# Sums of the exponentials in a second attention layer: one running tile, and the product with ones and the division each a step later

## The chip, the cores and the metric

The kernel runs on one core of one Trainium2 chip. The metric is the device time in microseconds (us), smaller is better. A time is a median of runs; beside it stands one profiled execution, from which all durations come.

## What is computed

Two cross-attention layers, in fp32, over 4 batches of 1024 rows of width 512. Cut to what matters here, layer 1 is:

```python
xn = x * rsqrt(mean(x * x) + 1e-5) * norm_w
q = rotate(xn @ wq)            # 16 heads of 32
k, v = rotate(ctx @ wk), ctx @ wv
q, k = q / norm(q), k / norm(k)
attn = softmax(q @ k.T * sqrt(32))
out = x + (attn @ v) @ wout
```

Since q and k are normalised, no maximum is subtracted: the kernel takes exp(scores), multiplies by v, and divides at the end by the sum of the exponentials over all 1024 keys. That sum, for each query and head, is what the change is about. Layer 0 (16 heads of 64) is not edited.

## The kernel before, in words

The program is one long order of instructions for the engines, written out by hand: TensorE (PE) for all products and transposes, ScalarE (ACT) for exponentials and for most copies out of PSUM, VectorE (DVE) for maxima, adds, rotations and divisions, GpSimd (POOL) for small powers and some products, SyncE (SP) for transfers. Each engine works through its instructions in the order in which the code issues them; between engines there are semaphore waits.

The batches follow each other, and in each layer 0 comes before layer 1. PE's free time in an attention step is filled with other products, called units here: a queue `Units` holds functions with estimated costs, `fill(us)` runs so many of them, and a few due times (`until`) force them.

Layer 1 has, for each batch, two halves (of 8 heads each) of 8 blocks; a block is 256 queries (`qb`) of 4 heads (`g`), and has 4 steps (`kk`), each for 256 keys. A half so has 32 steps, a batch 64, and the kernel 64 blocks. `Attention1.step` (from L594) does, in this order:

- 16 score matmuls (L599, four heads side by side in the array) into two PSUM tiles; there are two such buffers, both used by one step, so that the scores of the next step wait for the exponentials of this one.
- two exponentials on ACT (L609) into `self.e[:, kk % 2]`; the tile has two places, so an exponential waits until the product and the adds of two steps ago have read its place.
- `self.finish()` (L611): the division left over from before, and `product` of the step before: 8 value matmuls (L638) into the PSUM tile `av` (tag f0). At a block's end it adds 8 matmuls with a tile of ones (L649), for the running sum and for the last pair-sum, into the second half of the same PSUM bank. One ACT copy (L653) takes both halves out; the division (reciprocal L656, product L657) is left for the next step.
- `self.u.fill(us)`: units. In a first half these are the projections of q, k and v of layer 1 with their transposes; in a second half the output of layer 1 (`po`) and the next batch's preparation.
- on DVE, two adds (L615), which add the two key tiles of a step's exponentials, into `both[:, kk]`, and for kk = 1 and 2 a running add (L619) into `both[:, 0]`.

The function `bank` gives a unit one of three PSUM banks in turn during layer 1 (f1 to f3). A unit that gets a bank waits until what was in it has been read. A q or k projection is read by ACT (a square, L499) and by DVE (L501 to L503), which with L504 and L506 are called the rotation here; then POOL (L508, L512) finishes it and a transpose follows two chains later (L521). The function `post` runs at once in layer 1, so the rotation stands on DVE ahead of the adds of the step in which the projection ends.

In the last batch's second half the blocks are sorted so that o[2] is complete first, and the products with the last half of `wout` (`adds`) are put into the queue at fixed steps; what is left runs after the loop (`tail`).

Of the kernel before, what the change touches and what calls it, by code (L numbers as in the profile page):

```python
# [30 lines left out]
F32 = mybir.dt.float32  # L31
# [4 lines left out]
P = 128  # L36
S = 1024
NT = S // P
# [8 lines left out]
HD1 = 32  # L47
# [60 lines left out]
def xattn_kernel(ctx: ExitStack, tc: tile.TileContext, a: dict, out: bass.AP):  # L108
    nc = tc.nc
# [6 lines left out]
    ps_f = ctx.enter_context(tc.tile_pool(name="ps_f", bufs=1, space=bass.MemoryType.PSUM))  # L116
# [7 lines left out]
    def bank(name):  # L124

        which["n"] = which["n"] + 1 if which["n"] < 3 else which["from"]
        return ps_f.tile([P, 512], F32, tag=f"f{which['n']}", name=name)
# [7 lines left out]
    ones = const.tile([P, HD1], F32, name="ones")  # L135
# [224 lines left out]
    class Attention0:  # L360


        def __init__(self, b, units):
            self.b, self.u = b, units
            self.blocks = deque()
# [209 lines left out]
    WQ = 256  # L575

    class Attention1:


        def __init__(self, b, units):  # L580
            self.b, self.u = b, units
            self.last = None
            self.av = None
            self.quotient = None
            self.e = sb.tile([P, 2, 2, 2, 2, WQ], F32, tag="e", bufs=2, name=f"e1_{b}")
            self.both = sb.tile([P, 4, 4, WQ], F32, tag="big", bufs=2, name=f"both_{b}")
            rest = sb.tile([P, 4, 1024], F32, tag="big", bufs=2, name=f"rest_{b}")
            self.avs = rest[:, 0].rearrange("p (n c q) -> p n c q", n=2, c=2)
            v1 = rest[:, 2:].rearrange("p g (t f) -> p g t f", f=P)
            self.v1 = [v1[:, g] for g in range(2)]  # L590

        def step(self, half, g, qb, kk, kT, qT, v, o, us):
            n = f"{self.b}_{half}_{g}_{qb}_{kk}"
            sc = [score(f"s1_{n}_{u}", (P, 2, 2, WQ)) for u in range(2)]  # L594
            for c in range(2):
                for j in range(4):
                    rr = slice(j * HD1, (j + 1) * HD1)
                    k = 2 * kk + c
                    nc.tensor.matmul(  # L599
                        sc[j // 2][:, j % 2, c, :],  # L600
                        kT[rr, g, k * P : (k + 1) * P],
                        qT[rr, g, qb * WQ : (qb + 1) * WQ],
                        start=True,
                        stop=True,
                    )
            es = []
            for u in range(2):
                e = self.e[:, kk % 2, u]
                nc.scalar.activation(e, sc[u], AF.Exp, scale=float(np.sqrt(np.float32(HD1))))  # L609
                es.append(e)  # L610
            self.finish()  # L611
            self.last = (half, g, qb, kk, v, es, o)
            self.u.fill(us)
            for u in range(2):
                nc.vector.tensor_add(  # L615
                    self.both[:, kk, 2 * u : 2 * u + 2, :], es[u][:, :, 0, :], es[u][:, :, 1, :]
                )
            if 0 < kk < NT // 2 - 1:
                nc.vector.tensor_add(self.both[:, 0], self.both[:, 0], self.both[:, kk])  # L619

        def finish(self):

            if self.quotient is not None:
                self.quotient()
                self.quotient = None
            if self.last is not None:
                self.product()

        def product(self):
            half, g, qb, kk, v, es, o = self.last  # L630
            n = f"{self.b}_{half}_{g}_{qb}"
            if kk == 0:
                self.av = ps_f.tile([P, 2, WQ], F32, tag="f0", name=f"av1_{n}")
            first, end = kk == 0, kk == NT // 2 - 1
            for c in range(2):
                for j in range(4):
                    rr = slice(j * HD1, (j + 1) * HD1)
                    nc.tensor.matmul(  # L638
                        self.av[rr, 0, :],
                        v[g][:, 2 * kk + c, rr],  # L640
                        es[j // 2][:, j % 2, c, :],
                        start=first and c == 0,
                        stop=end and c == 1,
                    )
            if end:
                for i in (0, NT // 2 - 1):
                    for j in range(4):
                        rr = slice(j * HD1, (j + 1) * HD1)
                        nc.tensor.matmul(  # L649
                            self.av[rr, 1, :], ones, self.both[:, i, j], start=i == 0, stop=i > 0  # L650
                        )
                s = self.avs[:, qb % 2]
                nc.scalar.copy(s, self.av)  # L653

                def divide():
                    nc.vector.reciprocal(s[:, 1, :], s[:, 1, :])  # L656
                    nc.vector.tensor_mul(o[g][:, qb * WQ : (qb + 1) * WQ], s[:, 0, :], s[:, 1, :])  # L657

                self.quotient = divide
            self.last = None  # L660


# [5 lines left out]
    def flat(lists):  # L668
        return [u for lst in lists for u in lst]
# [54 lines left out]
    work = Units()  # L724
# [15 lines left out]
    tail = []  # L740
    for b in range(B):
# [6 lines left out]
        for p in range(NPAIR):  # L748
# [15 lines left out]
            elif p % 2 == 0:  # L764
                i = p // 2 - 1
# [4 lines left out]
                    lambda n, i=i: wo[i][:, n % 2, :],  # L770
# [29 lines left out]
            for i in range(NT):  # L800
# [8 lines left out]
                n = NT * (NPAIR - p if later else 1) - i  # L809
# [30 lines left out]
        att1 = Attention1(b, work)  # L840
# [10 lines left out]
        for half in range(2):  # L851
            n = 0
            if half == 0:
                vs = value_chains(att1.v1, wv1, ct, f"pv1_{b}_1")
                first = [q[1], (norms[1]["stats"], [], []), vs[0], (norms[1]["apply"], [], k1[1][2]), k1[2]]
                rest = [(norms[1]["turn"] + q[2][0], [], q[2][2]), k1[3], q[3], q1[0], vs[1], q1[1], q1[2]]
                rest += [q1[3], vs[2], vs[3]]
                chains = first + rest
                work.add(weave(chains, 2))
                def mark(c):  # L860

                    i = chains.index(c)
                    return sum(len(x[0]) for x in chains[: i + 3]) + sum(len(x[2]) for x in chains[: i + 1])

                base = work.done
                marks = {8: base + mark(q[1]), 16: base + mark(rest[0]), 24: base + mark(q[3])}
            else:
                for g in range(2, 4):
                    o[g] = sb.tile([P, S], F32, tag="vals", bufs=4, name=f"o1_{b}_{g}")
                wo1 = [wo_load(a["wout"], i, f"wo1_{b}_{i}") for i in range(2)]  # L870
                adds = add_units(xt, lambda n: o[n], lambda n: wo1[0][:, n % 2, :], f"po1_{b}_0", (0, 1))
                if b + 1 < B:
                    st, order = prepare_units(b + 1)
                    work.add(order(adds))
                else:
                    work.add(flat(adds))
            blocks = [(qb, g) for qb in range(S // WQ) for g in range(2)]
            final = b == B - 1 and half == 1
            if final:
                blocks.sort(key=lambda block: block[1])  # L880
                adds = [
                    add_units(
                        xt, lambda n: o[n], lambda n: wo1[1][:, n % 2, :], f"po1_{b}_{i}", (i,), store if i == 3 else None
                    )
                    for i in (2, 3)
                ]
            for qb, g in blocks:
                for kk in range(NT // 2):
                    if half == 0 and n in marks:
                        work.until(marks[n])  # L890
                    if final and n == 18:
                        work.add(flat(adds[0]))
                    if final and n in (22, 26, 30):
                        work.add(flat(adds[1][(n - 22) // 2 : (n - 18) // 2]))
                    att1.step(half, g, qb, kk, kT, qT, v, o[2 * half :], work.total() / (32 - n))
                    n += 1
            work.drain()
            kT, qT, v = kT1, qT1, att1.v1
        att1.finish()
        att1.quotient()  # L900
        which["from"], which["cols"] = 0, 1
        if b == B - 1:
            tail = flat(adds[1][6:])
        else:
            outs = add_units(
                xt, lambda n, o=o: o[n], lambda n, w=wo1[1]: w[:, n % 2, :], f"po1_{b}_1", (2, 3), store
            )
            tail = flat(outs)
# [38 lines left out]
```

## Time and profile before

| what | value |
|---|---|
| median of 3 runs (lowest, highest) | 2992.65 us (2991.08, 2992.93) |
| profiled execution: time, span | 2989.95 us, 2987.7 us |
| granted PE clock in it, mean | 0.996 |
| steps of layer 1, first half of batch 0 | 511.4 to 643.3 us |
| steps of layer 1, second half of batch 0 | 643.3 to about 775 us |
| steps of layer 1, last half of the last batch | 2864.5 to about 2974 us |

How to read it: the span is the time of the profiled execution between its first and last instruction. A row of a group gives the line in the code, engine, operation, output<-input, shapes and count, then the busy time in us, the mean of one in ns, and the engine's idle time just before these with what ended it. PEld is the load of weights, beside PE. A matmul in fp32 is two records. In the timeline a row has start, length, engine, line and operation, and in brackets the idle time of its engine before it. In the sums by stretch the values are the length, the busy time of each engine with its number of instructions, the granted clock, and the transfers. In a row of waits stand the sum, the number and the longest.

### The profile page before, as it was taken

The numbers are of one execution on the slowest core, as the hardware profiler recorded it, in microseconds if no ns is written. First come the engines' busy times: TensorE is split into PE (matmuls) and PEld (weight loads), VectorE is DVE, ScalarE is ACT, GpSimd is POOL, SyncE is SP. The second block draws the span as 40 slices with busy tenths as digits, with TensorE's granted clock in tenths as the row PEclk, the third lists the DMA queues.
The fourth block names the chain that finished last, engine by engine and source line by source line (L and its number), as shares of the span: only waits on it lengthen the run. The fifth ranks groups of instructions, "written<-read, shape, count | busy, mean of one in ns | idle before, by whom it ended". The sixth has DMA issues, their size and how long they took to land.

```text
span 2987.7 us, 60793 instructions
## 1 busy us (share of the span) xinstructions
PE 2917.3 (98%) x24748; PEld 1544.2 (52%) x24748; DVE 2230.7 (75%) x2824; ACT 1429.5 (48%) x2265; POOL 416.6 (14%) x392
## 2 busy tenths in 40 slices
PE   8999999999999999999999999999999999999998
PEld 5544546555544555655554454555455445455544
DVE  4777795877777779587777777958777777795777
ACT  3444443666443444465644344446664444444664
POOL 0010022420000002232000000223200000022310
PEclk9999999999999999999999999999999999999999
DMA  5788674010387867301048776730104978772000
GB/s 148 169 192 180 158 178 112 22 35 25 81 203 185 186 163 171 94 21 35 25 98 207 175 183 166 171 84 21 35 25 113 205 176 182 170 169 69 2 2 30
DMA packets 374134, 348.50 MB, mean 117 GB/s; under 512 B 37600, under 2 KB 355296, under 8 KB 373856
## 3 DMA queue, kind: packets, MB, share of 16 engines
q1 hardware_dynamic: 371664, 343.43, 48.4%
q8 instruction: 197, 3.23, 0.5%
q10 hardware_dynamic: 2192, 1.19, 0.2%
q14 instruction: 81, 0.66, 0.1%
HBM read 67.64 MB, written 8.39 MB: 25 GB/s over the span
## 4 chain that ended last, share of the span: by engine, by line
PE 78%; DVE 10%; DMA 4%; SPq 3%; ACT 2%; issue 1%; POOL 1%; DVEq 0%; ACTq 0%
PE s L372 14%; PE av L451 13%; PE po L158 10%; PE pv L158 7%; PE s L599 7%; PE av L638 6%; PE pqT L158 6%; PE pkT L158 5%; PE q_p L158 3%; DMA eT<-e 2%; SPq L406 2%; PE av L649 2%; DVE both L615 2%; DVE e L399 2%; PE k_p L158 1%; DVE m L393 1%
## 5 line engine op out<-in xcount | busy, mean ns | idle before, releaser
L394 ACT ACTIVATE e<-s,m 128x1024 f32<-128x1024 f32 x512 | 565.6, 1109 | 679.2 <-DVE m L393 613.8
L393 DVE TENSOR_REDUCE m<-s 128x1 f32<-128x1024 f32 x512 | 602.8, 1219 | 320.0 <-PE s L372 320.0
L399 DVE STREAM_TRANSPOSE e<-e 128x1024 f32<-128x1024 f32 x512 | 606.7, 1224 | 54.9 <-ACT e L394 43.0
L609 ACT ACTIVATE e<-s 128x1024 f32<-128x1024 f32 x512 | 496.5, 1022 | 315.1 <-PE s L599 300.1
L372 PE MATMUL s<-qk 64*128 64x512 f32 x2048 | 520.5, 615 | 6.0 <-ACT e L394 5.3
L451 PE MATMUL av<-eT,v 128*64 128x256 f32 x4096 | 474.8, 385 | 15.6 <-DMA eT<-e 13.7
L615 DVE TENSOR_TENSOR both<-e 128x512 f32<-128x512 f32 x512 | 342.4, 701 | 127.7 <-ACT e L609 92.5
L451 PEld LDWEIGHTS av<-eT,v 128*64 128x64 f32 x4096 | 289.4, 138 | 214.0 <-issue 53.7
L372 PEld LDWEIGHTS s<-qk 64*128 64x128 f32 x2048 | 181.8, 186 | 262.6 <-issue 188.9
L599 PE MATMUL s<-q,k 32*128 32x256 f32 x4096 | 305.7, 402 | 5.8 <-ACT q L526 2.7
L599 PEld LDWEIGHTS s<-q,k 32*128 32x128 f32 x4096 | 191.6, 185 | 149.7 <-ACT e L609 71.4
L158 PE MATMUL po<-wo,vals 128*128 128x512 f32 x512 | 239.6, 601 | 2.5 <-ACT v L130 2.5
L158 PE MATMUL pqT<-hT,w 128*128 128x512 f32 (+1 forms) x800 | 241.3, 597 | 0.7 <-ACT hT L255 0.7
L443 ACT COPY vals<-rT 128x256 f32<-128x256 f32 x128 | 47.7, 372 | 327.4 <-PE rT L442 327.4
L301 DVE TENSOR_TENSOR x<-x,po 128x512 f32<-128x512 f32 x200 | 133.8, 679 | 82.8 <-PE po L158 82.8
L158 PEld LDWEIGHTS pv<-w,cT 128*128 128x128 f32 (+1 forms) x2400 | 176.7, 152 | 30.3 <-issue 27.2
L158 PE MATMUL pv<-w,cT 128*128 128x128 f32 (+1 forms) x2400 | 186.5, 275 | 0.0
L158 PE MATMUL pkT<-cT,w 128*128 128x512 f32 (+1 forms) x600 | 181.6, 599 | 1.1 <-ACT cT L130 1.1
L619 DVE TENSOR_TENSOR both<-both 128x1024 f32<-128x1024 f32 x128 | 159.7, 1248 | 4.4
L158 PEld LDWEIGHTS po<-wo,vals 128*128 128x128 f32 x512 | 90.9, 190 | 106.4 <-issue 101.4
L158 PEld LDWEIGHTS pqT<-hT,w 128*128 128x128 f32 (+1 forms) x800 | 85.9, 151 | 112.2 <-issue 105.9
L638 PE MATMUL av<-e,v 128*32 128x256 f32 x2048 | 137.0, 385 | 0.0
(461 smaller groups left out, 2667.0 us busy)
## 6 DMA issues: line engine op xcount, KB each, us to landing
eT<-e SPq DMA_DIRECT2D x2048, 128.0 KB, 2.8
xr<-in_x_dram SPq DMA_DIRECT2D x32, 256.0 KB, 4.3
x<-in_x_dram SPq DMA_DIRECT2D x32, 256.0 KB, 3.8
wo<-in_Wo_dram SPq DMA_DIRECT2D x16, 512.0 KB, 4.2
out_dram<-x SPq DMA_DIRECT2D x32, 256.0 KB, 2.7
w<-in_Wq_dram SPq DMA_DIRECT2D x31, 256.0 KB, 4.0
c<-in_ctx_dram SPq DMA_DIRECT2D x32, 192.0 KB, 4.5
wkv<-in_wkv_dram SPq DMA_DIRECT2D x16, 384.0 KB, 3.5
```

What stands on the lines that cost most here:

```text
L158: nc.tensor.matmul(o[rr], lhsT[:, rr], rhs, start=start, stop=stop)
L301: nc.vector.tensor_add(xt[t], xt[t], pp[0])
L372: nc.tensor.matmul(sc[j][:, kb * 512 : (kb + 1) * 512], pr["qT"][r[j], i * P : (i + 1) * P], pr["kT"][r[j], kb * 512 : (kb + 1) * 512], st ...
L393: nc.vector.tensor_reduce(m[:, j : j + 1], sc[j], AX.X, ALU.max, negate=True)
L394: nc.scalar.activation(e[j], sc[j], AF.Exp, bias=m[:, j : j + 1], accum_out=l[:, j : j + 1])
L399: nc.vector.transpose(e[j], e[j])
L451: nc.tensor.matmul(av[r[j], :W].rearrange("p (t a i) -> p t a i", t=BQ, a=4), pr["v"][:, k, r[j]], eT[:, j, :, :, k * 32 : (k + 1) * 32], ...
L599: nc.tensor.matmul(sc[j // 2][:, j % 2, c, :], kT[rr, g, k * P : (k + 1) * P], qT[rr, g, qb * WQ : (qb + 1) * WQ], start=True, stop=True,)
L609: nc.scalar.activation(e, sc[u], AF.Exp, scale=float(np.sqrt(np.float32(HD1))))
L615: nc.vector.tensor_add(self.both[:, kk, 2 * u : 2 * u + 2, :], es[u][:, :, 0, :], es[u][:, :, 1, :])
L619: nc.vector.tensor_add(self.both[:, 0], self.both[:, 0], self.both[:, kk])
L638: nc.tensor.matmul(self.av[rr, 0, :], v[g][:, 2 * kk + c, rr], es[j // 2][:, j % 2, c, :], start=first and c == 0, stop=end and c == 1,)
```

## The change

- At each step the two pair-adds go into a tile `part` (into `total` at the block's first step), and at each later step, the last one too, `part` is added to `total`. `total` and `part` alternate between two places by blocks. A block so has three running adds instead of two.
- The product with ones takes `total` alone: 4 matmuls instead of 8. It isn't in the block's last `product` any more, but a function `sums`, called by `finish` a step later, ahead of that step's value product. It writes into a bank that `bank` gives, one of the three of the units, and a second ACT copy takes it out.
- The division follows a step after that.
- `av` has a bank to itself, and its copy takes only the values.
- In the last half the products of the last output begin two steps later, and four, not two, units of the last group come after the loop. Three calls of `finish` end a batch.

```diff
@@ step
             self.finish()
             self.last = (half, g, qb, kk, v, es, o)
             self.u.fill(us)
+            total, part = (self.both[:, 2 * (self.n % 2) + i] for i in range(2))
             for u in range(2):
-                nc.vector.tensor_add(
-                    self.both[:, kk, 2 * u : 2 * u + 2, :], es[u][:, :, 0, :], es[u][:, :, 1, :]
-                )
-            if 0 < kk < NT // 2 - 1:
-                nc.vector.tensor_add(self.both[:, 0], self.both[:, 0], self.both[:, kk])
+                to = (part if kk else total)[:, 2 * u : 2 * u + 2, :]
+                nc.vector.tensor_add(to, es[u][:, :, 0, :], es[u][:, :, 1, :])
+            if kk:
+                nc.vector.tensor_add(total, total, part)
@@ finish
             if self.quotient is not None:
                 self.quotient()
                 self.quotient = None
+            if self.sums is not None:
+                self.sums()
+                self.sums = None
             if self.last is not None:
                 self.product()
@@ product
             if end:
-                for i in (0, NT // 2 - 1):
-                    for j in range(4):
-                        rr = slice(j * HD1, (j + 1) * HD1)
-                        nc.tensor.matmul(
-                            self.av[rr, 1, :], ones, self.both[:, i, j], start=i == 0, stop=i > 0
-                        )
                 s = self.avs[:, qb % 2]
-                nc.scalar.copy(s, self.av)
+                nc.scalar.copy(s[:, 0, :], self.av[:, :WQ])
+                total = self.both[:, 2 * (self.n % 2)]
+                self.n += 1
 
                 def divide():
                     nc.vector.reciprocal(s[:, 1, :], s[:, 1, :])
                     nc.vector.tensor_mul(o[g][:, qb * WQ : (qb + 1) * WQ], s[:, 0, :], s[:, 1, :])
 
-                self.quotient = divide
+                def sums():
+                    ps = bank(f"sums_{n}")
+                    for j in range(4):
+                        rr = slice(j * HD1, (j + 1) * HD1)
+                        nc.tensor.matmul(ps[rr, :WQ], ones, total[:, j], start=True, stop=True)
+                    nc.scalar.copy(s[:, 1, :], ps[:, :WQ])
+                    self.quotient = divide
+
+                self.sums = sums
@@ xattn_kernel, layer 1
-                    if final and n == 18:
+                    if final and n == 20:
                         work.add(flat(adds[0]))
-                    if final and n in (22, 26, 30):
-                        work.add(flat(adds[1][(n - 22) // 2 : (n - 18) // 2]))
+                    if final and n in (24, 28):
+                        work.add(flat(adds[1][(n - 24) // 2 : (n - 20) // 2]))
@@
-        att1.finish()
-        att1.quotient()
+        for _ in range(3):
+            att1.finish()
@@
-            tail = flat(adds[1][6:])
+            tail = flat(adds[1][4:])
```

More of the change, by code (lines that the diff above doesn't have):

```diff
@@ L583, in __init__ @@
             self.av = None
-            self.quotient = None
+            self.sums = self.quotient = None
+            self.n = 0
             self.e = sb.tile([P, 2, 2, 2, 2, WQ], F32, tag="e", bufs=2, name=f"e1_{b}")
@@ L632, in product @@
             if kk == 0:
-                self.av = ps_f.tile([P, 2, WQ], F32, tag="f0", name=f"av1_{n}")
+                self.av = ps_f.tile([P, 2 * WQ], F32, tag="f0", name=f"av1_{n}")
             first, end = kk == 0, kk == NT // 2 - 1
@@ L638, in product @@
                     nc.tensor.matmul(
-                        self.av[rr, 0, :],
+                        self.av[rr, :WQ],
                         v[g][:, 2 * kk + c, rr],
```

## The prediction

> **What bounds the kernel now.** I read the page's first part, then the sums by stretch, then the groups of instructions and the waits of PE, and last the timeline around the longest of those waits.
>
> ```profile
> PE 2917.3 (98%) x24748; PEld 1544.2 (52%) x24748; DVE 2230.7 (75%) x2824; ACT 1429.5 (48%) x2265; POOL 416.6 (14%) x392
> ```
>
> PE sets the time over the whole span. The change touches layer 1 only, so I look there: first half of batch 0, its second half, and the second half of the last batch (us, then the busy time of PE, PEld, DVE, ACT, POOL).
>
> ```profile
> 511.00:645.00 134.00, 127.52 (x1940) 71.87 (x1944) 102.86 (x144) 83.89 (x112) 48.28 (x31) 0.99 0.06 17
> 645.00:777.00 132.00, 131.73 (x1960) 69.24 (x1952) 93.65 (x129) 81.88 (x99) 3.74 (x4) 1.00 0.13 39
> 2866.00:2987.00 121.00, 111.73 (x1408) 52.99 (x1400) 93.44 (x122) 66.92 (x73) 0.00 (x0) 0.99 0.05 19
> ```
>
> A second half with a next batch has no idle PE; a first half has 6.5 us, the last one 9.3. DVE, at 77%, 71% and 77%, is the second engine. What the change edits (all lines), and PE's waits:
>
> ```profile
> L615 DVE TENSOR_TENSOR both<-e 128x512 f32<-128x512 f32 x512 | 342.4, 701 | 127.7 <-ACT e L609 92.5 <-PE av L649 35.2
> L619 DVE TENSOR_TENSOR both<-both 128x1024 f32<-128x1024 f32 x128 | 159.7, 1248 | 4.4
> L656 DVE RECIPROCAL rest<-rest 128x256 f32<-128x256 f32 x64 | 111.9, 1748 | 11.3 <-ACT rest L653 9.9
> L649 PE MATMUL av<-both,ones 128*32 128x256 f32 x1024 | 80.3, 383 | 15.4 <-DVE both L615 15.4
> ```
>
> ```profile
> PE av L649 <- DVE both L615: 15.4, 9, 2.2
> ...
> PE pth L253 <- DVE rot L503: 6.7, 4, 1.7
> ```
>
> The first is the wait that the change aims at, the second a wait for a filler bank that DVE still reads. Step 28 of the first half of batch 0 (counted from 0, it starts at 623.76) shows how the first comes about:
>
> ```profile
> 625.23 0.68 DVE L501 TENSOR_TENSOR rot<-q_p,cos 128x512 f32<-128x512 f32 x1
> ...
> 627.82 2.51 DVE L615 TENSOR_TENSOR both<-e 128x512 f32<-128x512 f32 x4
> ...
> 628.56 1.24 PE L649 MATMUL av<-both,ones 128*32 128x256 f32 x6 [2.22 <-DVE both L615]
> ```
>
> And the sums by stretch for the time just after it (the value after POOL's is PE's granted clock):
>
> ```profile
> 630.00:632.00 2.00, 2.00 (x24) 1.50 (x17) 1.44 (x2) 0.58 (x1) 1.92 (x2) 0.50 0.00 0
> ```
>
> A rotation stands on DVE ahead of the adds; the sums product waits; and PE then runs at half clock, 0.50. Step 28 takes 8.65 us (623.76 to 632.40). Its work is 4.22: from starts in an undisturbed step (543.88, 544.95, 545.84, 546.70), scores 1.07, product 0.88, sums product 0.86, and three filler groups of 0.47. So 4.4 us are lost.
>
> [...] a gap of 2.22 us suffices here: of nine PE gaps over 2.1 us in the timeline, six are followed by half clock; none of 1.67 or less is. A drop costs 1.7 us. [...] each rotation on DVE (L501) starts just after ACT's square (L499) ends, 559.69 and 559.76 for one. [...] L619's typical one takes 1225. [...] the L619 at 620.90, beside POOL's L512, took 1.95 us.
>
> **The change part by part.** A batch has 64 steps, 32 per half, and a block is four; the sums of a block fall 7 times in a first half and 9 times in a second, its end included (L649 has 112 and 144 records there, 16 each).
>
> *Sums product, 8 matmuls to 4.* 0.86 to 0.43 us: a first half saves 3.0, a second 3.9. All of it is on PE.
>
> *Third running add per block.* 64 x 1.225 = 78 us on DVE, 9.8 per half: DVE would be busy 113 us in a first half whose PE work is about 118. It lies beside PE work only as long as DVE is not late.
>
> *Sums a step later.* The wait on the last pair-add goes, and DVE no longer waits for L649 (35.2 us). In its place the sums wait for the whole running total, queued behind whatever DVE has. Behind them on PE wait the value product and all fillers.
>
> *Division another step later.* Same 2.17 us, now at the third step of a block, ahead of that step's rotation and adds.
>
> *Copies.* One of 0.586 becomes two of 0.38 (L568's 128x256 form): ACT +0.17 x 64 = 11 us. ACT is at 62%; if that cover fails, a square behind the copy starts 0.4 later, which I count at step 17 below.
>
> *The sums take a filler bank.* Three banks go round. The order in which the built program issues instructions shows PE waits on DVE and ACT that were not there, where a sum comes between two projections: the second transpose of step 6, the value projection of step 17, the second q projection of step 22 now ask for the bank of a projection that has just ended.
>
> *Last half.* Output units start two steps later and four, not two, run after the last step, with their adds and stores on DVE and SP; the first two now fill PE's 3.02 us wait for the last division.
>
> First half, walked by hand from the trace's durations (adds 1.25 per step, running add 1.15, rotation 2.6, division 2.1, as they follow each other on DVE), in us:
> - Step 4 waits for POOL's rotation at 529.43 in any case: the 0.86 saved there is lost again, +0.86.
> - Step 6: bank free 5.26 into the step, PE there at 2.97: 2.3 (before 1.65).
> - Step 12: 2.5 before, gone. But DVE then holds division, three pair-adds, three running adds and two rotations in a row; the total of step 11 ends at about 567.1, the sums of step 13 are reached at 564.1: 3.0.
> - Steps 16, 20, 28: 0.84, 0.42 and 4.43 before, gone.
> - Step 17: product and sums end the projection at 584.96, the transpose ends at 585.55, the rotation has read the bank at about 587.4: 1.85, new. Step 22: 604.13 against 606.03: 1.9, new. Step 29: sums late by 0.7.
>
> Before 9.83, after 9.75 + 0.86 = 10.6. With the 3.0 of work a first half gains 2.2; four, 9. The 9.83 hold their lost clock; the new ones do not. I give a drop 0.75 for step 13, 0.4 for step 6, 0.15 each for 17 and 22: 1.45 x 1.7 = 2.5, times four: 10 back. Bounds: no drop, or all 16, 27 us. First halves: **+1**.
>
> Second halves with a next batch: 3.9 less 0.9 for bank waits and for the total at the batch's end (it ends at 774.41, where the product before it ends near 774.1): 3.0 x 3 = **-9** (bounds -12 and -4).
>
> Last half: steps 0 to 19 are paced from exponential to exponential, and each block's L649 lies in a pace (4.19 instead of 3.32); the four sums moved lie under a 2.77 pace that has room. 5 x 0.87 = 4.4, and less to wait in the first block 0.2. In the last twelve steps (2929.5 to 2974.3, 44.8) PE work falls by 3 x 0.43 + two units of 0.87 = 3.0; DVE there needs about 42.7, near the bound. The tail loses about 0.1 by the running add against the filled gap. **-7.5** (bounds -10 and -2).
>
> Sum: 1 - 9 - 7.5 = -15.5. Against the profiled execution (2989.95, span 2987.7): 2974.5. The median of the runs is 2.7 above that execution, so **2977**.
>
> **Rivals.** *The total is in time.* If DVE, freed of its waits for L649, is early by 3 us at step 13, the waits of 13 and 29 go. Speaks for it: 31 us idle DVE in a first half. Against: at that place DVE is gapless from 552 to 565 already. Per first half 10.6 - 3.7 = 6.9 against 9.83, and 3.0 of work: -5.9, four -24, no drops; with -16.5: 2952.
> *The bank wait becomes the bound.* DVE's queue doesn't drain, each of the 12 bank waits grows by one running add, 12 x 1.225 = 15, and every wait costs clock, 27: -9 + 42 - 16.5 = +16.5, so 3009. It decides from the point where a first half waits, clock included, over 7 us more than before. For it: three waits lie at 1.85 to 2.3, close to the 2.1 from which clock is lost. Against: 1.67 cost none.
> *Nothing changes.* Waits only move, and the 0.43s go into exponentials' pace: 2992.
>
> **Chances.** Forecast 0.50 (of this 0.36 faster, 0.10 same, 0.04 slower; its own range 2966 to 2996), total in time 0.24, bank wait 0.22, nothing 0.04. About 0.2% (6 us) is what a measurement of this kernel can tell from no change. Faster 0.60, same 0.14, slower 0.26. Range 2948 to 3010: it takes in the middle of the two rivals and leaves some 0.08 below and 0.10 above.
>
> **What would show it.** L649's successor with 512 records and waits of PE for the running add (3 us at step 13, not at step 12); new PE waits on L503 of about 2 us at steps 17 and 22; DVE above 110 us in a first half; half clock after step 13. It would be wrong if no PE wait on L503 appears beside step 6, if DVE is never a step behind, or if second halves don't shorten by 3 us each.

## The result, and the profile after

The changed kernel takes 3011.24 us, the median of seven runs (3001.69 to 3015.06). Seven runs of the kernel before, made beside them on the same chip, give 2991.10 (2988.97 to 2997.24). The medians are 20 us apart; the ratio over all runs is 1.0051, interval 1.0035 to 1.0068, which is 15 us. It is slower, where I had forecast 15 us less. The seven runs of the changed kernel lie in two groups, three near 3002 and four from 3011 to 3015, and the profiled one (3013.35) is of the upper group.

The first part of the page after shows the work that was taken from PE and given to DVE: 524 PE records fewer (512 of the sums; 12 because two more output units run after the loop, as one matmul each instead of four), 64 more DVE instructions, 83 us more DVE work. (A matmul is two records; a step has 8 score matmuls in 16 records, not 16 matmuls as said above.)

```profile
PE 2911.9 (97%) x24224; PEld 1537.8 (51%) x24224; DVE 2313.5 (77%) x2888; ACT 1428.6 (47%) x2329; POOL 421.8 (14%) x392
```

The sums by stretch come next: the first half of batch 0, its second half, and the end of the last batch (length, busy time of PE, PEld, DVE, ACT and POOL, granted clock, transfers).

```profile
514.00:652.00 138.00, 124.93 (x1856) 69.73 (x1856) 112.55 (x150) 82.22 (x117) 49.12 (x31) 0.95 0.05 16
652.00:782.00 130.00, 128.60 (x1908) 67.50 (x1906) 103.82 (x138) 82.77 (x110) 3.74 (x4) 1.00 0.12 35
2889.00:3011.00 122.00, 111.82 (x1380) 53.62 (x1372) 107.10 (x134) 69.90 (x87) 0.00 (x0) 0.97 0.05 19
```

The second half got shorter and has hardly any idle PE. The first half got longer: PE is idle for 13 us of it, and its granted clock is 0.95, where it was 0.99. The following table sets the stages of the two profiled executions side by side. A stage's length is taken from one step's start to the next in the trace; "half" is the time in it that the clock stands at half.

| stage | before, us | half | after, us | half | difference |
|---|---|---|---|---|---|
| layer 0, four batches | 1941.4 | 10.2 | 1949.0 | 27.2 | +7.6 |
| first halves, four | 526.4 | 10.2 | 552.8 | 58.1 | +26.4 |
| second halves, three | 396.7 | 0 | 389.4 | 0 | -7.3 |
| last half with the tail | 123.2 | 3.9 | 119.9 | 8.6 | -3.3 |

So most of the loss lies in the first halves. Three things make up the 26.4 us there. PE is idle for 51.7 us (length less busy time), where it was for 24.2: 27.5 more. PE is busy for 52.7 of the 58.1 us at half clock, where it was busy for all of the 10.2; the clock is 0.50 there, and the value product takes 1.93 us instead of 1.07 (both below). If half of the busy time is lost, this is up to 21 us more, an estimate from these numbers. What is left of the sum, about 22 us, is work that PE was spared; 12 of it are the four products of 28 blocks (0.43 us each), and where the rest comes from was not traced. So the new waits alone take up the gain, and the clock makes it a loss.

The groups of instructions that the change made, by shape:

```profile
L618 DVE TENSOR_TENSOR both<-e 128x512 f32<-128x512 f32 x512 | 345.4, 706 | 92.2 <-ACT e L610 87.3
L620 DVE TENSOR_TENSOR both<-both 128x1024 f32<-128x1024 f32 x192 | 237.4, 1236 | 6.6
...
L663 PE MATMUL sums<-both,ones 128*32 128x256 f32 x512 | 43.4, 413 | 26.1 <-DVE both L620 26.1
```

The sums product is halved (512 records, 43.4 us, where L649 had 1024 and 80.3), and DVE no longer waits for PE ahead of a pair-add: the 35.2 us put down to L649 are gone from the row of L618. In their place the row of L663 has 26.1 us of idle PE. The waits of PE (sum, number, longest) put it in order:

```profile
PE sums L663 <- DVE both L620: 26.1, 16, 4.4
PE q_t L521 <- POOL rot L512: 9.4, 4, 2.3
...
PE pth L253 <- DVE rot L503: 7.9, 4, 2.0
PE q_p L158 <- DVE rot L503: 7.9, 4, 2.0
PE pv L158 <- DVE rot L503: 7.3, 4, 1.8
```

Before, the first and the last two rows didn't exist; L649's 15.4 stood in their place, the third was 6.7 and the second 2.3. Each of the last four comes once per first half, always at the same step. The timeline around the longest wait of a first half, step 13 of batch 0, shows how it comes about:

```profile
562.84 1.75 DVE L656 RECIPROCAL rest<-rest 128x256 f32<-128x256 f32 x1
...
567.09 1.23 DVE L620 TENSOR_TENSOR both<-both 128x1024 f32<-128x1024 f32 x1
...
568.24 0.68 DVE L501 TENSOR_TENSOR rot<-k_p,cos 128x512 f32<-128x512 f32 x1
...
570.82 1.28 DVE L618 TENSOR_TENSOR both<-e 128x512 f32<-128x512 f32 x2
...
572.13 1.22 DVE L620 TENSOR_TENSOR both<-both 128x1024 f32<-128x1024 f32 x1
...
573.41 1.08 PE L663 MATMUL sums<-both,ones 128*32 128x256 f32 x8 [3.74 <-DVE both L620]
...
574.27 1.93 PE L642 MATMUL av<-e,v 128*32 128x256 f32 x16
```

Among what follows on DVE are a division, a running add, a rotation, a pair-add and the third running add of the block. The sums stand for 3.74 us at the head of PE's queue, and the value product that comes behind them then takes 1.93 instead of 1.07. The sums by stretch of the same place show the clock (the value after POOL's):

```profile
572.00:579.00 7.00, 5.58 (x56) 2.56 (x56) 6.93 (x8) 1.93 (x3) 3.99 (x2) 0.52 0.00 0
```

The clock is 0.52: half clock began at 572.3, inside the wait, and lasted 6.83 us. Step 13 takes 11.19 us in all.

### The profile page after: what moved, and what is told of

It reads as the page before. It is cut to its first block, busy times and chain, and to the rows that moved or that the text cites. A ratio compares the mean times of both kernels' runs of the same rounds, so it can differ in the third digit from the quotient of the medians.

```text
span 3011.1 us, 59861 instructions
## 1 busy us (share of the span) xinstructions
PE 2911.9 (97%) x24224; PEld 1537.8 (51%) x24224; DVE 2313.5 (77%) x2888; ACT 1428.6 (47%) x2329; POOL 421.8 (14%) x392
## 4 chain that ended last, share of the span: by engine, by line
PE 76%; DVE 12%; DMA 4%; ACT 3%; SPq 2%; issue 2%; POOL 1%; ACTq 0%; DVEq 0%
PE s L372 14%; PE av L451 13%; PE po L158 10%; PE s L600 7%; PE pv L158 7%; PE pqT L158 6%; PE av L642 6%; PE pkT L158 4%; PE q_p L158 3%; DMA eT<-e 2%; DVE both L618 2%; DVE both L620 2%; PE k_p L158 2%; SPq L406 2%; DVE e L399 1%
## 5 line engine op out<-in xcount | busy, mean ns | idle before, releaser
L618 DVE TENSOR_TENSOR both<-e 128x512 f32<-128x512 f32 x512 | 345.4, 706 | 92.2 <-ACT e L610 87.3
L600 PE MATMUL s<-q,k 32*128 32x256 f32 x4096 | 313.6, 408 | 4.5 <-ACT q L526 2.7
L620 DVE TENSOR_TENSOR both<-both 128x1024 f32<-128x1024 f32 x192 | 237.4, 1236 | 6.6
L158 PEld LDWEIGHTS pv<-w,cT 128*128 128x128 f32 (+1 forms) x2400 | 176.7, 152 | 30.3 <-issue 27.2
L642 PE MATMUL av<-e,v 128*32 128x256 f32 x2048 | 145.4, 404 | 0.0
```

The costliest lines, as they stand in the source:

```text
L158: nc.tensor.matmul(o[rr], lhsT[:, rr], rhs, start=start, stop=stop)
L600: nc.tensor.matmul(sc[j // 2][:, j % 2, c, :], kT[rr, g, k * P : (k + 1) * P], qT[rr, g, qb * WQ : (qb + 1) * WQ], start=True, stop=True,)
L618: nc.vector.tensor_add(to, es[u][:, :, 0, :], es[u][:, :, 1, :])
L620: nc.vector.tensor_add(total, total, part)
L642: nc.tensor.matmul(self.av[rr, :WQ], v[g][:, 2 * kk + c, rr], es[j // 2][:, j % 2, c, :], start=first and c == 0, stop=end and c == 1,)
```

## The experiments

Theory A says that the turn of the filler banks is the cause: the sums take one of three banks that go round, so all units behind them come back to a bank one unit earlier, while DVE still reads it. Theory B says that the late total is the cause: the third running add, on an engine that has fallen behind, stands at the head of PE's queue. None of the kernels below leaves out a part of the computation. The first four were made with 35 runs of the kernel before (median 2991.84), the last four with 11 (2988.67); the ratios are to these.

**The sums out of the turn.** The kernel after, but the sums use the bank that is next without moving the turn on.

```diff
                 def sums():
+                    kept = which["n"]
                     ps = bank(f"sums_{n}")
+                    which["n"] = kept
```

> The changed kernel, but the sums' bank doesn't move the turn of the three filler banks (the next unit takes the same bank). Theory A (the loss comes from PE gaps and the half clock after them; the gaps at steps 6, 17 and 22 of a first half from the shifted turn of banks): step 6 back to a gap of 1.7 us, no gaps on L503 at 17 and 22, no half clock after 6 and 17; per first half 0.3 + 1.8 + 2.0 + 3.4 = 7.5 us less, 30 in all, about 2980. Theory B (the loss is DVE's 78 us of added adds, the banks only show it): the waits move to the sums or the exponentials, time within 6 us of the changed kernel, 3003 to 3012.

Measured: 2994.51 us, ratio 1.0007 (0.9994 to 1.0020), so about 17 us of the 20 came back by the medians, 13 of 15 by the ratio. PE's waits in its profile:

```profile
PE sums L665 <- DVE both L620: 26.3, 20, 4.4
...
PE pth L253 <- DVE rot L503: 6.2, 4, 1.5
...
PE q_p L158 <- ACT rest L666: 3.4, 4, 0.9
```

The bank waits of steps 17 and 22 are gone, that of step 6 is back to 1.5, and a small new one appears, of a unit that takes the bank which ACT still copies the sums from (0.86 us each). The wait for the total is untouched, at 3.74 in step 13, and so is the half clock after it. So A's part is worth most of the net loss. B may still be worth more than the few us that are left, because the loss is net of the work that PE was spared.

**Two running adds.** The kernel after, with the third running add left to PE: the sums are eight products again, four of `total` and four of `part`.

```diff
-            if kk:
+            if 0 < kk < NT // 2 - 1:
                 nc.vector.tensor_add(total, total, part)
@@ product
-                total = self.both[:, 2 * (self.n % 2)]
+                total, part = (self.both[:, 2 * (self.n % 2) + i] for i in range(2))
@@ sums
-                        nc.tensor.matmul(ps[rr, :WQ], ones, total[:, j], start=True, stop=True)
+                        nc.tensor.matmul(ps[rr, :WQ], ones, total[:, j], start=True, stop=False)
+                    for j in range(4):
+                        rr = slice(j * HD1, (j + 1) * HD1)
+                        nc.tensor.matmul(ps[rr, :WQ], ones, part[:, j], start=False, stop=True)
```

> The changed kernel with two running adds per block, as before, and 8 products with ones (running sum, last pair-sum) in the filler bank a step later. Theory A: PE has 28 us more of work, the wait for the total at step 13 shrinks to about 1 us and loses its half clock, step 4's late transpose is 0.9 earlier, the bank gaps at 6, 17 and 22 stay: about as the changed kernel, 3000 to 3010. Theory B: all gaps go with the adds, 28 us of work come back, and the waits of before are gone too: 2960 to 2985.

Measured: 2996.51 us, 1.0006 (0.9991 to 1.0020): between what A and what B had given. PE's waits:

```profile
PE q_p L158 <- DVE rot L503: 7.9, 4, 2.0
PE pth L253 <- DVE rot L503: 7.9, 4, 2.0
...
PE pv L158 <- DVE rot L503: 6.4, 4, 1.6
PE sums L666 <- DVE both L618: 6.2, 5, 1.3
PE q_t L521 <- POOL rot L512: 5.7, 4, 1.4
```

The bank waits stand much as in the kernel after (1.98, 1.61 and 1.98 at steps 6, 17 and 22), the wait for the sums falls from 26.1 to 6.9 us (6.2 and 0.7 of another row), and three of the four first halves have no half clock at all (131.0 us each). The second halves don't gain (132.3 to 133.2), as PE's work there is the old one. So B is a second part.

**The sums later in the step.** The kernel after, with the sums issued at the end of the step, behind its value product and its fillers, and ahead of its adds. `finish` only hands the function over as `due`, and a new `settle` (its few lines are left out here) calls it after `self.u.fill(us)` and after each `finish` at a batch's end.

```diff
             self.u.fill(us)
+            self.settle()
@@ finish
-            if self.sums is not None:
-                self.sums()
-                self.sums = None
+            self.due, self.sums = self.sums, None
```

> The changed kernel with the sums' product issued at the end of the step, after its fillers and before its adds, instead of ahead of the value product. Theory A: the wait for the total at step 13 (3.7 us) shrinks by product and fillers, 2.3 us, and its two stretches of half clock go (3.4 us lost per first half); bank gaps stay or move: about 23 us less, 2980 to 2992. Theory B: DVE is no less late, the exponentials wait instead: 3003 to 3012.

Measured: 2995.08 us, 1.0008 (0.9997 to 1.0018), 16 us less than after. A row of its waits:

```profile
PE sums L668 <- DVE both L621: 8.9, 8, 4.1
```

The wait of step 13 falls from 3.74 to 0.96, all waits for the total from 26.1 to 8.9 us, of which 4.1 is the tail's. Bank waits stay: steps 6 and 22 at 1.97 and 1.98; at step 17 the sums themselves wait for their bank, 1.41; and the value projection of step 27 now waits 2.35. A q projection of step 15 waits 1.71 for ACT. So the part of B is smaller once the waiting sums stand behind other work, even with the third add on DVE.

**One tile, without the delay.** The kernel before with the third running add and four products at the block's end, in `av`'s bank: neither the turn of banks nor the division moves.

```diff
-            if 0 < kk < NT // 2 - 1:
+            if kk:
                 nc.vector.tensor_add(self.both[:, 0], self.both[:, 0], self.both[:, kk])
@@ product
-                for i in (0, NT // 2 - 1):
-                    for j in range(4):
-                        rr = slice(j * HD1, (j + 1) * HD1)
-                        nc.tensor.matmul(
-                            self.av[rr, 1, :], ones, self.both[:, i, j], start=i == 0, stop=i > 0
-                        )
+                for j in range(4):
+                    rr = slice(j * HD1, (j + 1) * HD1)
+                    nc.tensor.matmul(self.av[rr, 1, :], ones, self.both[:, 0, j], start=True, stop=True)
```

> The kernel before with one part of the change alone: three running adds and 4 products with ones, at the block's end in av's bank, no delay. Theory A: no bank gaps; PE work 28 us less, but the wait of the sums' product grows by one add (1.2 us) at steps 12, 16, 20 and 28, and clock is lost after 12 and 28: 4 x (4.9 + 1.7 to 3.4) = 26 to 33 more; 2988 to 2998. Theory B: the added adds alone make the loss, 3003 or more.

Measured: 3032.98 us, 1.0134 (1.0115 to 1.0153). A missed here by 35 us or more; B, 3003 or more, held. One row of its waits says all:

```profile
PE av L648 <- DVE both L619: 79.1, 41, 4.5
```

The wait for the sums grew from 15.4 us in 9 places to 79.1 in 41, in second halves too. Without the delay of a step the third add costs far more than the four products that it saves. The delay is the useful part of the change, as the first row of the last table shows: there two adds and eight products stay, and the delay with a bank outside the turn is 0.4% faster than before.

**The turn alone.** The kernel before, where each division also moves the turn of banks on by one; the bank that is passed over stays unused. Nothing else is changed, and not one instruction is added.

```diff
                 self.quotient()
                 self.quotient = None
+                which["n"] = which["n"] + 1 if which["n"] < 3 else which["from"]
```

> The kernel before, but the turn of the filler banks moves on by one bank, left unused, at each division: the bank part of the change alone, with no work added. Theory A: the waits on L503 at 6, 17 and 22 appear: per first half 0.3 + 1.8 + 2.0 us, and up to two stretches of half clock (3.4): +16 to +30, 3007 to 3021, with the waits of L649 partly shortened by them. Theory B (DVE's added adds are the cause): within 5 us of before, 2987 to 2997.

Measured: 3009.81 us, 1.0069 (1.0057 to 1.0081), as A had said. PE's waits:

```profile
PE av L650 <- DVE both L615: 15.5, 9, 2.2
PE pth L253 <- DVE rot L503: 8.4, 4, 2.1
PE q_p L158 <- DVE rot L503: 7.9, 4, 2.0
PE pv L158 <- DVE rot L503: 7.9, 4, 2.0
```

The first row is that of the kernel before. The other three add 0.4, 2.0 and 2.0 us to a first half, 17.5 us over four, and the four first halves are 16.0 us longer than before (542.4 against 526.4) with 10.2 us of half clock as before, though after steps 6 and 22, where the kernel before had it after step 28. So in this execution the turn alone costs its waits and no more clock than before: a loss as large as that of the change, from a bank that nothing is written to.

**The parts together.** Three more kernels join the edits above: the sums out of the turn with two running adds; the sums out of the turn and late in the step; and all three. Their diffs are those above, put together.

> The changed kernel with the sums outside the turn of the filler banks, and with two running adds and 8 products with ones. Each of these alone brought the changed kernel (3011) to about 2995. Theory A (PE's gaps and the half clock after them add up, place by place): no gaps on L503 at 17 and 22, the wait at 13 at 1.3 us, no half clock in first halves: first halves 127 to 129 us, second halves as with two adds, 132.5; about 2980. If both cure the same loss: 2993 again.

> The changed kernel, sums outside the turn of the filler banks and issued at the end of the step. Theory A: gaps at 17 and 22 go, the wait at 13 is about 1 us; first halves 127 to 130 us, second halves 129 to 130 as with the sums at the step's end; about 2965 to 2972. If DVE's load is the bound: first halves stay at 133 or more and it is 2985 or more.

> As the one with the sums at the step's end and outside the turn, but with two running adds and 8 products with ones. Theory A: no wait for the sums at all, first halves 127 to 129, second halves 132 to 133: 2975 to 2982, slower than with three adds by the 28 us of products less what DVE still costs.

| edits to the kernel after | us | ratio to before | interval |
|---|---|---|---|
| out of the turn, two adds | 2979.11 | 0.9962 | 0.9950 to 0.9974 |
| out of the turn, late | 2970.77 | 0.9939 | 0.9926 to 0.9952 |
| out of the turn, late, two adds | 2963.99 | 0.9914 | 0.9902 to 0.9926 |

The first two came as expected. The third missed: I had expected it above the second, since PE has 3 us more to do per first half, and it is 7 us below. Each of the three edits alone takes about 0.0044 off the ratio of after (1.0051). Out of the turn with two adds takes off 0.0089, as much as the two alone, so the turn and the late total are separate losses. Out of the turn and late takes off 0.0112, more than the two alone (0.0087): with them go also the waits at steps 15 and 27 (1.71 and 2.35) that the kernel with late sums alone had. Two adds on top of these take off only 0.0025 more, since both they and the later place act on the wait for the total (26.1 us in after, 8.6 in the second kernel, 1.1 in the third). The third kernel is faster than both kernels of the case, and it has as many products and adds as the kernel before the change. Its first half of batch 0, by the sums by stretch, and two of the largest waits that remain in first halves:

```profile
511.00:638.00 127.00, 122.58 (x1933) 69.45 (x1930) 102.84 (x143) 83.47 (x118) 46.97 (x30) 1.00 0.06 17
```

```profile
PE pth L253 <- DVE rot L503: 6.2, 4, 1.5
...
PE sums L670 <- DVE rot L503: 5.6, 4, 1.4
```

The granted clock is 1.00, DVE is back at 103 us (112.55 in after's first half), and no wait of a first half is over 1.54 us. Its four first halves take 126.2 us each, where those of the kernel before take 130.4 to 132.1 and those of after 137.7 to 139.3; they have no half clock, and those of the second kernel of the table have 23.9 us of it in all. My expectation that the third would be slower than the second had no term for clock.

## Why the prediction was wrong

**The waits of a first half: right, place by place.** They came where the walk had put them. Predicted against measured, in us: step 6 2.3 and 1.98; step 13 3.0 and 3.74; step 17 1.85 and 1.82; step 22 1.9 and 1.97; step 29 0.7 and 1.02. The waits of steps 12 and 28 went, DVE has 112.55 us in a first half (I said 113), and a block's product with ones takes PE 0.46 us (0.43).

**The clock: the term that failed.** The step was "I give a drop 0.75 for step 13, 0.4 for step 6, 0.15 each for 17 and 22: 1.45 x 1.7 = 2.5, times four: 10 back". In the four first halves half clock came after step 13 four times of four and each time for 6.83 us, after step 17 four times of four, after step 6 three times, after step 4, to which I had given no chance, twice, and after step 22 never. These are 13 stretches, nine of 3.41 us and four of 6.83, 58.1 us together, which by the same estimate cost up to 29 us instead of 10 (26 for the 52.7 us in which PE is busy). The 1.7 for a drop was an estimate too, half of the 3.41 us that each of the three stretches in the first halves of before lasts (628.61 to 632.02 for one). Both the sum and its upper bound had counted one stretch of 3.41 for a drop at step 13, where each took two. My chances rested on one sentence, that no gap of 1.67 or less in the trace of before is followed by half clock. That held for that trace, but in after a gap's length alone doesn't tell: step 17 with 1.82 lost clock four times of four, step 22 with 1.97 not once in four.

In the kept traces the loss goes with where the gap lies on a grid in time. In all ten traces every one of the 192 changes of the granted clock falls, within 6 ns, on a grid of 3413.3 ns, which runs through the whole trace (the 13 of before and the 39 of after within 3 ns). Where the program's first instruction falls in a window of the grid differs from trace to trace, from 0.05 to 0.98 of it. The gap of step 17 in after lies inside one window in all four batches. That of step 22 is cut by a border, into 1.30 and 0.67 us in batch 0. The sums by stretch of these windows (length, PE, PEld, DVE, ACT, POOL, clock, transfers), the window of step 17's gap, the next, and the two of step 22's gap:

```profile
592.74:596.16 3.42, 1.60 (x24) 0.73 (x19) 2.32 (x6) 1.68 (x4) 0.00 (x0) 1.00 0.00 0
596.16:599.57 3.41, 3.41 (x32) 1.85 (x36) 3.38 (x5) 1.50 (x2) 2.76 (x2) 0.50 0.00 0
613.22:616.64 3.42, 2.12 (x32) 1.10 (x28) 3.16 (x5) 2.91 (x4) 0.00 (x0) 1.00 0.00 0
616.64:620.05 3.41, 2.74 (x44) 1.59 (x48) 3.34 (x7) 0.99 (x2) 1.39 (x2) 1.00 0.02 5
```

In the first halves of all ten traces, of the windows at full clock in which PE was idle for less than 1.73 us, 0 of 1401 are followed by a window at half clock; from 1.73 to 1.98 us, 20 of 27; from 1.98 us on, 31 of 31. (The ends of matmuls are modelled, so these limits are rough.) In the first halves of before and after alone, all 16 windows followed by half clock had 1.82 us or more, and the two with most idle PE that weren't had 1.77 and 1.81, both in after. The trace of before had it already: of its four gaps of 2.22 us at step 28 only the one that a border cuts near its middle, into 1.22 and 1.00, lost no clock. So a chance by length alone was the wrong kind of term: of the gaps of 1.8 to 2.3 us at these steps those of step 17 (1.82, inside one window) lost clock and those of step 22 (1.97, cut by a border, in batch 0 into 1.30 and 0.67) didn't.

**Step 4: half missed.** "+0.86" was right for what waits for POOL's rotation and is lost again: with two running adds the wait of step 4 is 1.43, where it was 0.57. With three it is 2.34, and the timeline of after shows what adds 0.91:

```profile
530.89 1.23 DVE L620 TENSOR_TENSOR both<-both 128x1024 f32<-128x1024 f32 x1
531.07 1.96 POOL L512 TENSOR_TENSOR rot<-rot,q_r 128x512 f32<-128x512 f32 x1
...
533.08 0.66 PE L521 MATMUL q_t<-ident,rot 128*128 128x128 f32 x4 [2.34 <-POOL rot L512]
```

The third running add starts just ahead of POOL's product, which takes 1.96 us beside it, and the transpose waits for POOL. In before no DVE instruction runs beside it at this step, and it takes 1.05 (at 528.33). I had seen the two meet, but from the other side: in the L619 that took 1.95 us beside L512 at 620.90. I didn't ask where the new adds would meet L512. 4 x 0.91 = 3.6 us.

**The sum of the first halves.** Forecast +1, measured +26.4 in the profiled pair. By the estimate above the clock takes about 16 of the difference of 25.4 (21 less the 5 that the sum had), step 4 3.6, step 13 3.0 (4 x 0.74), step 29 1.3, and step 6 gives back 1.3: 22.6 in all. Where the other 3 us lie is open.

**Second halves: right.** -9 forecast, -7.3 measured, within -12 and -4.

**Last half: half right.** -7.5 forecast, -3.3 measured. Steps 0 to 19 gave 5.0 (forecast 4.6). The last twelve steps, up to the product after the loop (2974.28 before, 2994.96 after), gave only 1.0 where the sum had 3.0; why was not tried. The term for the tail, "loses about 0.1 by the running add", was wrong: from that product to the end it lost 2.7. PE's 3.02 us wait for the last division is gone, but the last sums wait 4.35 us for the total (at 3000.36), and half clock raises the stage's from 3.9 to 8.6 us, up to 2.3 of the loss:

```profile
3000.36 1.08 PE L663 MATMUL sums<-both,ones 128*32 128x256 f32 x8 [4.35 <-DVE both L620]
```

**The rivals.** "The total is in time" fell with step 13. "The bank wait becomes the bound" gave 3009, 2 us from the result, but only one half of it holds. Every wait costing clock, 27 us, is close to the 29 measured, but not place by place: step 22 cost none and step 13 double. Bank waits growing by a running add each, 15 us, didn't occur: they stayed at 1.8 to 2.0. What it lacked was made up by step 4, step 13, the tail and layer 0, so its closeness is in part luck.

**What stays open.** Layer 0 isn't touched by the change and is 7.6 us longer in this profile, with 17 us more of half clock, which would be up to 8.5 us. No term of mine covered it. Most likely it is chance: 2.8 us of it, with 6.8 us of half clock, lie in batch 0 ahead of the first edited instruction, and layer 0, the same in all ten kernels, takes from 1936.3 us (sums late in the step) to 1953.5 (two adds) in their profiles. The loss without it, 15.8 us in the profiled pair, is close to the 15 of the ratio. Each kernel has one kept trace, so whether the grid's place also makes the two groups of after's runs (mean clock 0.989 to 0.990, and 0.984 to 0.986) can't be seen. Not tried alone were the later start of the last output, and late sums with two adds in the turn of after.

## What to carry to other kernels

A small product that takes a buffer out of a shared turn can cost everyone else in the turn, as it did here (21 us for the turn alone): before giving it a place, walk the turn and see who comes back to a buffer that is still being read, and keep it out of the turn if it can be. Work that is moved from a full engine to one that is busy at three quarters is not free where an instruction waits for it at the head of the full engine's queue, as the sums did here for 26.1 us (8.9 later in the step): put the waiting instruction behind the step's other work, and check what it gained there by moving that alone. Where PE waits of about 2 us appear, count the clock for each of them in the range, and look at their place on the grid on which the trace's clock changes: before lost no clock after gaps of 1.67 us or less, nor after one of its four gaps of 2.22 at step 28, while after lost clock after each of its four gaps of 1.82 at step 17.

## What was not expected of the hardware

- In the profiles of before, after and the first four experiments, PE gaps over 0.8 us were followed by half clock, by length: under 1.2 us 0 of 26; 1.2 to 1.9 us 14 of 85; 1.9 to 2.1 us 10 of 33; 2.1 to 2.6 us 16 of 32; over that 30 of 34. A gap at the same step in each batch lost clock every time in one kernel (1.82 at step 17 of after, 4 of 4) and seldom in another (1.98 at steps 6 and 22 with two adds, 2 of 8). The idle time in one window of the 3413.3 ns grid parts them better: in the first halves of ten traces 1.98 us or more was followed by half clock 31 times of 31, less than 1.73 never. Outside the first halves there is one place with less, in layer 0, where half clock followed 1.32 us 16 times (three times in after, at 432.32, 1179.84 and 1923.94; a fourth window with 1.32, from 2667.97 on, was not followed by it).
- In after, POOL's product L512 (128x512) takes 1.95 to 1.97 us in all 13 places where it starts 0.17 to 0.18 us after a DVE add L620 (two 128x1024 operands in fp32). In before it takes 1.76 to 1.77 in the eight places where it starts 0.36 to 0.37 us after an L619 of that shape, and 1.05 where no DVE instruction runs beside it (528.33).
- Moving a turn of three banks on by one unused bank at each of 64 divisions cost 21 us of the median (3009.81 against 2988.67), 16 of it in the first halves of the profile, without one instruction more.
